# Layer 0's scores and queries as seven block products instead of eight (Strassen's form, float32)

## The chip, the core and the metric

The kernel runs on one core of a Trainium2 chip. The metric is device time in microseconds (us), the median of three runs. A core has five engines that run side by side, each its own queue in order: TensorE (PE in the profile) multiplies 128-wide blocks into PSUM, VectorE (DVE) and ScalarE (ACT) work element by element and can read PSUM, GpSimd (POOL) works on SBUF and reduces across partitions, SyncE (SP) issues transfers. They wait for each other by semaphores. All data here is float32.

## The reference, cut to what matters

Two attention layers on eight images of 1024 tokens and 256 channels:

```python
# layer 0: four heads, each 256 wide
qkv = einsum('bnc,cd->bnd', x, W_qkv)             # per head: q, k, v
atten = softmax(einsum('bihd,bjhd->bijh', q, k) * 256**-0.5, axis=j)
x = einsum('bijh,bjhd->bihd', atten, v) @ W_out + b_out + x
# layer 1: one head, keys and queries 32 wide, values 256 wide
f, g, h = x@Wf + bf, x@Wg + bg, x@Wh + bh
x = gamma * softmax(g @ f.T) @ h + x
```

## The kernel before

**Folding.** For each of layer 0's heads the kernel multiplies Wq by Wk transposed and Wv by W_out once (`fold_weights`). A query projection then gives Q = Wqk^T x^T, and the scores are x Q: the transposed tokens `x0T` serve as keys. The scores are kept transposed, keys on partitions and queries along the row.

**Blocks.** A head of an image is two blocks (`blk` 0 and 1) of 512 queries. A block's scores are eight key tiles of 128, each two products (channels 0 to 127 and 128 to 255) of 512 columns into one PSUM bank of the pool `ps_s`, four banks deep (L359). ScalarE copies each bank to the tile `s` (L367). VectorE takes the maximum over the key tiles (L373, L381, L383), GpSimd takes it across partitions (`partition_all_reduce`, L385), VectorE subtracts it in two instructions of 2048 elements (L388), and ScalarE takes the exponential (L391). Two blocks later, `values` multiplies the exponentials with V, four tasks of eight products of 257 columns (the last is the row sum, L402), and VectorE divides and adds to the rows (L410, L412). V has a column of ones, which GpSimd writes by a memset (L243).

**Order.** The heads of an image run one after the other; layer 1 of image b-1 stands after head 1 of image b (for the last image, after head 3), and layer 1 of the last image stands at the end. TensorE's order is fixed by `weave`, which spreads lists of tasks evenly over each other: a block's scores, the values of two blocks ago, and `coming`, the next head's preparation (transposes, folding, queries, V). The other engines' instructions are ordered by a scheduler, and each of their queues runs in that order. Loads of x go out on SyncE's queue, loads of weights on ScalarE's.

**Pools.** `sb1`, `sb2` and `sb3` give each tag one, two or three buffers; a tile waits until the readers of the tile whose buffer it takes are done. The rows x, the transposed xT, V and `s` have three, the queries q two.

Of the kernel before, what the change touches and what calls it, by code (L numbers as in the profile page):

```python
# [11 lines left out]
F32 = mybir.dt.float32  # L12
# [9 lines left out]
def kernel(  # L22
# [40 lines left out]

    nc = tc.nc
# [19 lines left out]
    sb3 = ctx.enter_context(tc.tile_pool(name="sb3", bufs=3))  # L84
    small = ctx.enter_context(tc.tile_pool(name="small", bufs=8))
# [8 lines left out]
    def load_x(b):  # L94
        t = sb3.tile([P, NT, C], F32, tag="rows", name=f"x_{b}")
        for k in range(NBLK):
            nc.sync.dma_start(
                t[:, ts(k, HT), :].rearrange("p t c -> p (t c)"), x_v[b][:, k, :]
            )
        rows[b] = t  # L100
# [36 lines left out]
    weights = {}  # L137

    def load_weights(h):
        w = sb1.tile([P, CC, 3 * C], F32, tag="wqkv", name=f"wqkv{h}")  # L140
        nc.scalar.dma_start(w, wqkv_v[:, :, ts(h, 3 * C)])
        wo = sb1.tile([P, CC, C], F32, tag="wout", name=f"wout{h}")
        nc.scalar.dma_start(wo, wout_v[:, ts(h, CC), :])
        weights[h] = w, wo

    def fold_weights(h):

        wT = []
        folded[h] = []

        def turn(i, what):
            w, _ = weights[h]
            pt = ps_m.tile([P, NB], F32, tag="pm", name=f"pw{what}_{h}")
            for d in range(CC):
                for c in range(CC):
                    nc.tensor.transpose(
                        pt[:, d * C + c * P : d * C + (c + 1) * P],
                        w[:, c, i * C + d * P : i * C + (d + 1) * P],
                        ident,
                    )  # L160
            t = sb1.tile([P, CC, C], F32, tag=f"w{what}T", name=f"w{what}T_{h}")
            copy_on(i, t.rearrange("p d c -> p (d c)"), pt)
            wT.append(t)

        def multiply(i, what):
            wqT, wkT, wvT = wT
            pm = ps_m.tile([P, NB], F32, tag="pm", name=f"p{what}_{h}")
            for c in range(CC):
                for d in range(CC):
                    nc.tensor.matmul(  # L170
                        pm[:, ts(c, C)],
                        lhsT=(wqT, wvT)[i][:, d, ts(c, P)],
                        rhs=wkT[:, d, :] if i == 0 else weights[h][1][:, d, :],
                        start=(d == 0),
                        stop=(d == CC - 1),
                    )
            t = const.tile([P, CC, C], F32, tag=f"{what}{h}", name=f"{what}{h}")
            copy_on(i, t.rearrange("p c e -> p (c e)"), pm)
            folded[h].append(t)

        tasks = [partial(turn, i, what) for i, what in enumerate(("q", "k", "v"))]
        tasks += [partial(multiply, i, what) for i, what in enumerate(("wqk", "wvo"))]
        return tasks


    xT_of = {}

    def transpose_rows(b, layer):


        def task(k, c):
            if (b, layer) not in xT_of:
                xT_of[b, layer] = sb3.tile([P, CC, N], F32, tag="xT", name=f"x{layer}T_{b}")
            pt = ps_m.tile([P, NB], F32, tag="pm", name=f"px{layer}_{b}_{k}_{c}")
            for t in range(HT):
                nc.tensor.transpose(  # L196
                    pt[:, ts(t, P)], rows[b][:, k * HT + t, ts(c, P)], ident
                )
            copy_on(c, xT_of[b, layer][:, c, ts(k, NB)], pt)

        return [partial(task, k, c) for k in range(NBLK) for c in range(CC)]
# [39 lines left out]
    def values_tile(name):  # L241
        v = sb3.tile([P, NT, CV], F32, tag="v", name=name)
        nc.gpsimd.memset(v[:, :, C : C + 1], 1.0)  # L243
        return v

    class Layer0:
        scale = SCALE

        def __init__(self, b, h):
            self.b, self.h, self.name = b, h, f"{b}_{h}"  # L250
            self.kchunks, self.together = CC, 1
            self.s = {}

        def start(self):
            self.q = sb2.tile([P, CC, N], F32, tag="q", name=f"q_{self.name}")
            self.v = values_tile(f"v_{self.name}")
# [11 lines left out]
        def prepare(self):  # L268
            b, h = self.b, self.h
            tasks = [self.start]  # L270
            if h == 0:
                tasks += transpose_rows(b, 0)
            if h not in folded:
                tasks += fold_weights(h)
            tasks += project_T(
                f"q_{self.name}", lambda: folded[h][0], C, lambda: xT_of[b, 0],
                lambda d, k, pm: copy_on(d, self.q[:, d, ts(k, NB)], pm),
            )
            tasks += project_rows(
                f"v_{self.name}", lambda: folded[h][1], lambda: xT_of[b, 0], self.store_v  # L280
            )
            return tasks

        def keys(self, c, j):
            return xT_of[self.b, 0][:, c, ts(j, P)]

        def queries(self, c, j, blk):
            return self.q[:, c, ts(blk, NB)]
# [4 lines left out]
    class Layer1:  # L293
        scale = 1.0

        def __init__(self, b):
            self.b, self.name = b, f"{b}_l1"
            self.kchunks, self.together = 1, P // CK
            self.s = {}

        def start(self):
            b = self.b
            self.f = sb1.tile([P, N], F32, tag="f", name=f"f_{b}")
            self.g = sb1.tile([P, N], F32, tag="g", name=f"g_{b}")
            self.v = values_tile(f"v_{self.name}")
# [8 lines left out]
        def prepare(self):  # L314
            b = self.b
            tasks = [self.start] + transpose_rows(b, 1)
            tasks += project_T(
                f"fg_{b}", lambda: wfg_sb, P, lambda: xT_of[b, 1], self.store_fg
            )
            tasks += project_rows(  # L320
                f"v_{self.name}", lambda: wh_sb, lambda: xT_of[b, 1],
# [5 lines left out]
            return tasks  # L327

        def keys(self, c, j):
            r = j % (P // CK)  # L330
            return self.f[ts(r, CK), ts(j, P)]

        def queries(self, c, j, blk):
            r = j % (P // CK)
            return self.g[ts(r, CK), ts(blk, NB)]
# [8 lines left out]
    def scores(a, blk):  # L344
        n = f"{a.name}_{blk}"
        half = NT // 2
        quart = NT // 4
        m = []

        def task(j0):  # L350
            if j0 == 0:
                a.s[blk] = sb3.tile([P, NT, NB], F32, tag="s", name=f"s_{n}")
            s = a.s[blk]
            js = range(j0, j0 + a.together)
            pms = {}
            for j in js:
                pms[j] = ps_s.tile([P, NB], F32, tag="ps", name=f"ps_{n}_{j}")
                for c in range(a.kchunks):
                    nc.tensor.matmul(  # L359
                        pms[j],  # L360
                        lhsT=a.keys(c, j),
                        rhs=a.queries(c, j, blk),
                        start=(c == 0),
                        stop=(c == a.kchunks - 1),
                    )
            for j in js:
                nc.scalar.copy(s[:, j, :], pms[j])  # L367
                if j % half == half - 1:
                    lo = j + 1 - half
                    t = sb1.tile(  # L370
                        [P, quart, NB], F32, tag=f"m{len(m)}", name=f"m{len(m)}_{n}"
                    )
                    nc.vector.tensor_tensor(  # L373
                        t, s[:, lo : lo + quart, :], s[:, lo + quart : lo + half, :], ALU.max
                    )
                    m.append(t)
            if js[-1] == NT - 1:
                softmax(s)

        def softmax(s):  # L380
# [5 lines left out]
            for k in range(2):  # L386
                part = s[:, ts(k, half), :]
                nc.vector.tensor_tensor(  # L388
                    part, part, cmax.unsqueeze(1).broadcast_to([P, half, NB]), ALU.subtract
                )  # L390
                nc.scalar.activation(part, part, AF.Exp, scale=a.scale)  # L391

        return [partial(task, j) for j in range(0, NT, a.together)]
# [42 lines left out]
    weave(order[0].prepare())  # L436
    due = []
    for i, a in enumerate(order):
        if isinstance(a, Layer0):
            if a.b == 0 and a.h + 1 < HEADS:  # L440
                load_weights(a.h + 1)
            if a.h == 1 and a.b + 1 < B:
                load_x(a.b + 1)
        coming = order[i + 1].prepare() if i + 1 < len(order) else []
        for blk in range(NBLK):
            n = len(coming) // NBLK
            now = values(*due.pop(0)) if len(due) == 2 else []
            weave(scores(a, blk), now, coming[blk * n : len(coming) if blk else n])
            due.append((a, blk))
    weave(values(*due[0]), final.prepare())  # L450
    weave([t for blk in range(NBLK) for t in scores(final, blk)])
# [36 lines left out]
```

## Time and profile before

| | |
|---|---|
| median of 3 runs | 2645.35 us (2644.98 to 2645.82) |
| the profiled execution | 2644.62 us |
| its span (first to last instruction) | 2642.7 us |
| mean granted TensorE clock | 0.998 |
| TensorE busy | 2609.2 us, 9648 products (each float32 product counts twice) |
| VectorE busy | 1072.0 us |
| ScalarE busy | 757.8 us |
| GpSimd busy | 150.1 us |
| layer 0's score products (L359) | 943.5 us |
| layer 0's query products (L210) | 239.1 us |
| layer 0's values products (L402) | 931.4 us |

The profile is of one execution. A row of its list of costliest groups names the line, the engine, the operation, the tiles out<-in, the shape and count; then come the busy time and the mean duration of one in ns, and after the second bar the time that the engine stood idle just before these instructions, with what ended that wait. TensorE's products overlap, so the busy time of a group is less than count times mean; the distance between starts in the timeline gives the rate. PE is the products, PEld the weight loads beside them. A row of the timeline gives start, duration and the instructions merged into it. "issue" is time in which an engine waited for nothing that the profile shows.

### The profile page before, as it was taken

What the parts mean: (1) busy time and instruction counts of PE and PEld (TensorE: products, weight loads), DVE (VectorE), ACT (ScalarE), POOL (GpSimd) and SP (SyncE); (2) the same over time, 40 slices, a digit from 0 to 9 for tenths busy, and PEclk for the clock granted to TensorE, in tenths of its full rate; (3) what the DMA queues carried; (4) which work ended last, traced back from release to release, by engine and by line L of the source; (5) the groups of instructions that cost most, each with busy time, mean ns of one, the idle gap of its engine ahead of it and who ended that gap; (6) DMA issues with size and microseconds to landing.
All of it is one profiled execution on the core that took longest, in us unless ns stands there. A gap on an engine that the chain in (4) does not pass through costs nothing.

```text
span 2642.7 us, 22461 instructions
## 1 busy us (share of the span) xinstructions
PE 2609.2 (99%) x9648; PEld 1772.3 (67%) x9648; DVE 1072.0 (41%) x1373; ACT 757.8 (29%) x985; POOL 150.1 (6%) x126
## 2 busy tenths in 40 slices
PE   7999999999999999999999999999999999999998
PEld 4666666666666666766667666676666766666676
DVE  2333335433354343433444343453334533333453
ACT  2322223322332223322233222332223322222332
POOL 0000000000000000000000000000000000000000
PEclk9999999999999999999999999999999999999999
DMA  3000000000000000000000000000000000000000
GB/s 105 17 0 0 0 1 1 8 24 0 1 0 9 24 1 0 1 8 24 0 1 0 8 24 0 0 1 32 0 0 1 1 16 0 1 0 1 0 1 32
DMA packets 8866, 23.06 MB, mean 9 GB/s; under 512 B 2112, under 2 KB 3648, under 8 KB 8768
## 3 DMA queue, kind: packets, MB, share of 16 engines
q1 hardware_dynamic: 6592, 17.44, 1.8%
q10 hardware_dynamic: 2176, 4.19, 0.5%
q8 instruction: 76, 1.25, 0.2%
q14 instruction: 22, 0.18, 0.0%
HBM read 13.24 MB, written 8.39 MB: 8 GB/s over the span
## 4 chain that ended last, share of the span: by engine, by line
PE 95%; DVE 2%; ACT 1%; POOL 1%; issue 1%; POOLq 0%; ACTq 0%
PE ps L359 33%; PE pa L402 32%; PE pr_v L230 8%; PE pa_l L402 8%; PE pm_q L210 8%; PE pr_v_l L230 2%; PE px L196 1%; DVE s_l L388 1%; PE pm_fg L210 1%; PE ps_l L359 1%; ACT s_l L367 1%; POOL cmax_l L385 1%; ACT s_l L391 1%; DVE m_l L381 0%; DVE m_l L373 0%
## 5 line engine op out<-in xcount | busy, mean ns | idle before, releaser
L359 PE MATMUL ps<-q,x0T 128*128 128x512 f32 x2048 | 943.5, 592 | 0.0
L402 PE MATMUL pa<-v,s 128*128 128x257 f32 x4096 | 931.4, 381 | 0.7 <-DVE x L412 0.7
L402 PEld LDWEIGHTS pa<-v,s 128*128 128x128 f32 x4096 | 776.7, 190 | 210.5 <-issue 112.9
L359 PEld LDWEIGHTS ps<-q,x0T 128*128 128x128 f32 x2048 | 385.3, 190 | 349.6 <-issue 332.3
L367 ACT COPY s<-ps 128x512 f32<-128x512 f32 x512 | 297.6, 582 | 1047.2 <-PE ps L359 1046.9
L388 DVE TENSOR_TENSOR s<-s,cmax 128x2048 f32<-128x2048 f32 x128 | 287.6, 2289 | 113.8 <-POOL cmax L385 113.8
L391 ACT ACTIVATE s<-s 128x2048 f32<-128x2048 f32 x128 | 244.8, 1913 | 290.1 <-DVE s L388 290.1
L410 DVE RECIPROCAL r<-pa 128x1 f32<-128x1 f32 x256 | 42.4, 165 | 619.0 <-PE pa L402 619.0
L373 DVE TENSOR_TENSOR m<-s 128x1024 f32<-128x1024 f32 x128 | 156.8, 1225 | 244.5 <-ACT s L367 244.5
L230 PE MATMUL pr_v<-wvo,x0T 128*128 128x256 f32 x1024 | 242.1, 380 | 2.9 <-ACT q L133 2.9
L402 PE MATMUL pa_l<-v_l,s_l 128*128 128x257 f32 x1024 | 233.8, 384 | 7.4 <-DVE x L412 7.4
L210 PE MATMUL pm_q<-x0T,wqk 128*128 128x512 f32 x512 | 239.1, 592 | 0.0
L230 PEld LDWEIGHTS pr_v<-wvo,x0T 128*128 128x128 f32 x1024 | 194.3, 190 | 62.9 <-issue 32.5
L402 PEld LDWEIGHTS pa_l<-v_l,s_l 128*128 128x128 f32 x1024 | 196.5, 192 | 57.4 <-issue 32.3
L385 POOL PARTITION_ALL_REDUCE cmax<-smax x64 | 115.6, 1806 | 1248.1 <-DVE smax L383 1197.0
L210 PEld LDWEIGHTS pm_q<-x0T,wqk 128*128 128x128 f32 x512 | 97.4, 190 | 91.3 <-issue 87.4
L412 DVE SCALAR_TENSOR_TENSOR x<-pa,r,x 128x256 f32<-128x256 f32 x256 | 123.8, 483 | 8.5
L410 DVE RECIPROCAL r_l<-pa_l 128x1 f32<-128x1 f32 x64 | 10.6, 167 | 215.4 <-PE pa_l L402 215.4
L367 ACT COPY s_l<-ps_l 128x512 f32<-128x512 f32 x128 | 65.9, 606 | 79.8 <-PE ps_l L359 79.8
L391 ACT ACTIVATE s_l<-s_l 128x2048 f32<-128x2048 f32 x32 | 61.2, 1912 | 94.0 <-DVE s_l L388 93.7
L388 DVE TENSOR_TENSOR s_l<-s_l,cmax_l 128x2048 f32<-128x2048 f32 x32 | 71.9, 2288 | 23.1 <-POOL cmax_l L385 23.1
L381 DVE TENSOR_TENSOR m<-m,m 128x1024 f32<-128x1024 f32 x64 | 78.4, 1225 | 2.2
(53 smaller groups left out, 780.4 us busy)
## 6 DMA issues: line engine op xcount, KB each, us to landing
x<-in_x_dram SPq DMA_DIRECT2D x16, 512.0 KB, 4.4
out_dram<-x SPq DMA_DIRECT2D x16, 512.0 KB, 2.6
wqkv<-in_L_conv_W_qkv_dram ACTq DMA_DIRECT2D x4, 768.0 KB, 4.4
wout<-in_L_conv_W_out_dram ACTq DMA_DIRECT2D x4, 256.0 KB, 2.7
wh_sb<-in_L_conv_Wh_dram SPq DMA_DIRECT2D x1, 256.0 KB, 2.8
bout_sb<-in_L_conv_b_out_dram SPq DMA_DIRECT2D x1, 128.0 KB, 7.2
bh_sb<-in_L_conv_bh_dram SPq DMA_DIRECT2D x1, 128.0 KB, 3.7
wfg_sb<-in_L_conv_Wf_dram SPq DMA_DIRECT2D x2, 32.0 KB, 6.6
```

Of the source, the lines that this page charges most:

```text
L210: nc.tensor.matmul(pm[:m], lhsT=w()[:, c, d * P : d * P + m], rhs=src()[:, c, ts(k, NB)], start=(c == 0), stop=(c == CC - 1),)
L230: nc.tensor.matmul(pm[:, ts(j, C)], lhsT=src()[:, c, ts(2 * t2 + j, P)], rhs=w()[:, c, :], start=(c == 0), stop=(c == CC - 1),)
L359: nc.tensor.matmul(pms[j], lhsT=a.keys(c, j), rhs=a.queries(c, j, blk), start=(c == 0), stop=(c == a.kchunks - 1),)
L367: nc.scalar.copy(s[:, j, :], pms[j])
L373: nc.vector.tensor_tensor(t, s[:, lo : lo + quart, :], s[:, lo + quart : lo + half, :], ALU.max)
L381: nc.vector.tensor_tensor(m[0], m[0], m[1], ALU.max)
L385: nc.gpsimd.partition_all_reduce(cmax, smax, P, bass_isa.ReduceOp.max)
L388: nc.vector.tensor_tensor(part, part, cmax.unsqueeze(1).broadcast_to([P, half, NB]), ALU.subtract)
L391: nc.scalar.activation(part, part, AF.Exp, scale=a.scale)
L402: nc.tensor.matmul(pm[:, : C + 1], lhsT=p[:, j, ts(ti, P)], rhs=v[:, j, : C + 1], start=(j == 0), stop=(j == NT - 1),)
L410: nc.vector.reciprocal(r, pm[:, C : C + 1])
L412: nc.vector.scalar_tensor_tensor(acc, pm[:, :C], r, acc, ALU.mult, ALU.add)
```

## The change

The products of layer 0's scores and queries are computed by Winograd's variant of Strassen's method. Both operands are cut into four blocks (tokens in halves and channels in halves; for the queries of a block, halves of 256), some sums of blocks are formed, seven block products are taken instead of eight, and the four output blocks are sums of these.

- `seven` is a group of three TensorE tasks. "one" takes products 1, 6 and 5 into three banks x, y and z; "two" adds product 2 to x and 7 to y; "three" adds product 4 to y and 3 to z. Between them ScalarE copies x (e1), and VectorE forms u2 and u3 from y and e1 and writes the outputs 22, 21 and 12 from a bank and e1, u2 or u3; output 11 is a ScalarE copy of x. A bank that gets a further product is read before it, so that product waits for the reader.
- A score block has two groups, each of two key tiles per half (28 products of 256 columns in all); a query projection is one group of products of 512 columns.
- The sums of operands are made on GpSimd: `sum_a` once an image on the transposed tokens (four instructions of 512 elements), `sum_b` once a head on the folded weights (128 elements) and once an image and head on the queries (512 elements).
- The maxima are taken per group (`Softmax.have`), and the subtraction and exponential go in four quarters of 1024 elements instead of two halves.
- The next head's queries run in the middle of block 1, V of a head is computed in its own two blocks, weights of all heads are loaded at the start into buffers of `s`, and heads 0 and 1 are folded before the first scores, 2 and 3 within the first block.
- The rows, xT and V have two buffers instead of three; x of the next image is loaded at head 3 instead of head 1.

```diff
-    def load_weights(h):
-        w = sb1.tile([P, CC, 3 * C], F32, tag="wqkv", name=f"wqkv{h}")
...
+    def load_weights(pair):
+        t = sb3.tile([P, NT, NB], F32, tag="s", name=f"w_{pair}").rearrange("p j i -> p (j i)")
...
+    def sum_a(eng, sums, a11, a12, a21, a22):
+        s1, s2, s3, s4 = sums
+        eng.tensor_tensor(s1, a21, a22, ALU.add)
+        eng.tensor_tensor(s2, s1, a11, ALU.subtract)
+        eng.tensor_tensor(s3, a11, a21, ALU.subtract)
+        eng.tensor_tensor(s4, a12, s2, ALU.subtract)
+
+    def sum_b(eng, sums, b11, b12, b21, b22):
+        t2, t3, t4 = sums
+        eng.tensor_tensor(t3, b22, b12, ALU.subtract)
+        eng.tensor_tensor(b12, b12, b11, ALU.subtract)
+        eng.tensor_tensor(t2, b22, b12, ALU.subtract)
+        eng.tensor_tensor(t4, b21, t2, ALU.subtract)
+
+    def seven(name, parts, operands, outs, after=None):
...
+        def bank(k):
+            banks[k] = ps_s.tile([P, NB], F32, tag="ps", name=f"ps{k}_{name}")
...
+        def add(dst, k, other):
+            nc.vector.tensor_tensor(dst, shaped(banks[k]), shaped(other), ALU.add)
+
+        def one():
+            for k, number in (("x", 1), ("y", 6), ("z", 5)):
+                bank(k)
+                product(k, number, True)
+            nc.scalar.copy(scratch("e1"), banks["x"])
+            add(shaped(scratch("u2")), "y", sbs["e1"])
+
+        def two():
+            product("x", 2)
+            product("y", 7)
+            nc.scalar.copy(outs["11"](), shaped(banks["x"]))
+            add(shaped(scratch("u3")), "y", sbs["e1"])
+            add(outs["22"](), "z", sbs["u3"])
+
+        def three():
+            product("y", 4)
+            product("z", 3)
+            add(outs["21"](), "y", sbs["e1"])
+            add(outs["12"](), "z", sbs["u2"])
+            if after is not None:
+                after()
+
+        return [one, two, three]
...
+            if layer == 0 and (k, c) == (NBLK - 1, CC - 1):
+                xT = xT_of[b, 0]
+                sums = sb2.tile([P, 4, HN], F32, tag="xs", name=f"xs_{b}")
...
+                sum_a(nc.gpsimd, (s1, s2, s3, s4), a11, a12, a21, a22)
...
     def values_tile(name):
-        v = sb3.tile([P, NT, CV], F32, tag="v", name=name)
+        v = sb2.tile([P, NT, CV], F32, tag="v", name=name)
         nc.gpsimd.memset(v[:, :, C : C + 1], 1.0)
...
+        def queries(self):
...
+            def after():
+                sums = sb2.tile([P, 3, NBLK, HB], F32, tag="qs", name=f"qs_{self.name}")
...
+                sum_b(nc.gpsimd, [sums[:, k] for k in range(3)], *blocks)
...
+        def have(self, pairs):
+
+            s, m, n = self.tile(), self.m, self.n
+            t = sb1.tile([P, 2, NB], F32, tag=f"m{len(m)}", name=f"m{len(m)}_{n}")
+            nc.vector.tensor_tensor(t, *[s[:, lo:hi, :] for lo, hi in pairs], ALU.max)
+            m.append(t)
+            if len(m) < 2:
+                return
             nc.vector.tensor_tensor(m[0], m[0], m[1], ALU.max)
...
             nc.gpsimd.partition_all_reduce(cmax, smax, P, bass_isa.ReduceOp.max)
-            for k in range(2):
-                part = s[:, ts(k, half), :]
+            for k in range(4):
+                part = s[:, ts(k, NT // 4), :]
...
+            fill = [values(*due.pop(0)) if len(due) == 2 else []]
+            n = len(own) // NBLK
+            fill.append(own[n:] if blk else own[:n])
+            if blk == 0:
+                fill.append(early)
+            elif isinstance(nxt, Layer0):
+                n = len(main) // 2
+                main = main[:n] + queries + main[n:]
+            else:
+                fill.append(queries)
+            weave(main, *fill)
             due.append((a, blk))
```

## The prediction

> **What bounds the kernel now.** I read the page's busy times first, then the chain that ended last, the costliest groups, and last the timelines of one stretch and of the start.
>
> ```profile
> PE 2609.2 (99%) x9648; PEld 1772.3 (67%) x9648; DVE 1072.0 (41%) x1373; ACT 757.8 (29%) x985; POOL 150.1 (6%) x126
> PE 95%; DVE 2%; ACT 1%; POOL 1%; issue 1%; POOLq 0%; ACTq 0%
> L359 PE MATMUL ps<-q,x0T 128*128 128x512 f32 x2048 | 943.5, 592 | 0.0
> L402 PE MATMUL pa<-v,s 128*128 128x257 f32 x4096 | 931.4, 381 | 0.7 <-DVE x L412 0.7
> L388 DVE TENSOR_TENSOR s<-s,cmax 128x2048 f32<-128x2048 f32 x128 | 287.6, 2289 | 113.8 <-POOL cmax L385 113.8
> L373 DVE TENSOR_TENSOR m<-s 128x1024 f32<-128x1024 f32 x128 | 156.8, 1225 | 244.5 <-ACT s L367 244.5
> ```
>
> TensorE is the bound: 95% of the chain, and 0.0 and 0.7 us idle before its two large groups. VectorE waits for others, so its order has cost nothing so far.
>
> The timeline of a score block, TensorE:
>
> ```profile
> 1048.12 3.63 PE L402 MATMUL pa<-v,s 128*128 128x257 f32 x16
> 1051.59 1.88 PE L359 MATMUL ps<-q,x0T 128*128 128x512 f32 x4
> 1053.30 1.88 PE L210 MATMUL pm_fg<-x1T,wfg_sb 128*128 128x512 f32 x4
> ...
> 1060.20 1.89 PE L230 MATMUL pr_v_l<-wh_sb,x1T 128*128 128x256 f32 x8
> 1061.93 3.60 PE L359 MATMUL ps<-q,x0T 128*128 128x512 f32 x8
> ```
>
> Start to start, a values task takes 3.47 us, four instructions of 512 columns 1.72, eight of 256 columns 1.73. A float32 product is two instructions: 0.86 us for 512 columns, 0.43 for 256. Halving the width costs nothing, so seven products for eight do save an eighth.
>
> VectorE and GpSimd in the softmax of that block:
>
> ```profile
> 1046.76 1.22 DVE L381 TENSOR_TENSOR m<-m,m 128x1024 f32<-128x1024 f32 x1
> 1048.02 0.69 DVE L383 TENSOR_TENSOR smax<-m 128x512 f32<-128x512 f32 x1
> 1049.04 1.16 DVE L312 COPY f<-f 64x512 f32<-64x512 f32 x1 [0.32 <-ACT f L311]
> 1050.90 4.50 DVE L388 TENSOR_TENSOR s<-s,cmax 128x2048 f32<-128x2048 f32 x2 [0.71 <-POOL cmax L385]
> 1055.43 0.42 DVE L312 COPY g<-g 64x512 f32<-64x512 f32 x1
> ```
>
> smax ends at 1048.71 and VectorE is free of the subtractions only at 1055.4. What stands behind them, in order, waits; here TensorE never needs it soon.
>
> GpSimd at the start:
>
> ```profile
> 0.87 0.19 POOL L243 MEMSET v<- 128x8 f32 x3
> 11.78 0.28 POOL masks.py:199 TENSOR_SCALAR_AFFINE_SELECT ident<-ident 128x128 f32<-128x128 f32 x1 [10.72 <-issue]
> ```
>
> The program has a library load of GpSimd between these two; the gap is 10.72 us.
>
> [...] The trace has 10.72 us, but from 2 to 8 us the DMA engines stood at 0.9 to 1.0 busy with the first loads. [...]
>
> **The change, part by part.**
>
> Removed: each of 64 score blocks runs 28 products of 256 columns for 16 of 512: two units of 0.86, 64 x 1.72 = 110.1 us. Each of 32 query projections runs seven for eight: 27.5 us. Sum 137.6 us of TensorE time. It is real only where TensorE doesn't wait.
>
> Added on VectorE: five PSUM sums per group of seven, five groups per head, 800 in all, at 690 ns (the row of L262, the nearest) 552 us, less 64 query copies (44 us). 1072 + 508 is about 1580 us in 2640: capacity is there. ScalarE loses copies. Neither is the bound on average; what counts is order.
>
> Where TensorE now waits: a group's tasks are "one" (2.58 us), "two" (1.72), "three" (1.72). "three" begins with product 4, accumulated into bank y, and so waits for u3, a VectorE sum. VectorE's stream has, in most blocks, u2 of the next block's first group, then the last maxima, smax, the four subtractions, and only then u3. So product 4 waits for the previous block's whole softmax. Take t=0 where the last values task before a block's end ends. After a matmul's slot VectorE starts 0.21 us later (30.73 to 30.94 at the start).
> TensorE: three to 1.72, one to 4.30, values to 7.77, two to 9.49; in block 1 a V projection (1.72) follows and product 4 is due at 11.2; in block 0 a values task, due at 12.96.
> VectorE: output 21 from 1.07 to 1.76, output 12 from 1.93 to 2.62, maximum (1.23) to 3.88, u2 to 4.6, maximum to 5.84, smax to 6.56. All-reduce from 6.73 (0.17 later, as in the trace) to 8.55 (1.8). Four subtractions (4.5 to 4.9) to 13.35. Reciprocal, u3 to 14.25; product 4 starts at 14.3. Then output 22, a values update and the exposed weight load (190 ns) add 0.5 to 0.8 before product 3.
> Wait: 3.6 us on entering block 1 (14.3 - 11.2 + 0.5), 2.0 on entering block 0.
>
> GpSimd's reloads: the sums (tensor_tensor) and the all-reduce are in two libraries. The built program's GpSimd stream has 39 loads ahead of an all-reduce and 38 back; before has one each. The loads back hide: the query sums wait for mid-block-1 anyway. The others don't. In block 1 the queue reads: four query sums, memset of the next V tile, load, all-reduce. V has two buffers now, so the memset waits for the last values task, t=0. The load starts near 0.3 and the all-reduce at 0.3+L in place of 6.73. At L=6 it is covered; at L=8 it costs 1.6 us; at 10.7, 4.3. This happens at 31 entries into a Layer-0 block 0.
> At seven heads (h=3, another image to come) four x sums stand ahead of block 0's all-reduce. Three of them follow the last transposed copy (t=0.8)[...], then the load[...].
>
> L is the unknown: [...] 10.7 (trace, DMA full). In mid-kernel the DMA is idle (8 GB/s)[...]. I take 8.
> Waits at L=8: 25 x 3.6 = 90, 7 x 10.1 = 71, 31 x 3.6 = 112; sum 273.
> Start: queries now wait for x sums, weight sums and query sums[...], against folds done early: +8. Seven entries into Layer 1, with copies queued behind exponentials: +10. [...]
> Span: 2642.7 - 137.6 + 273 + 28 = 2806. The profiled execution took 2644.6, 1.9 over its span, and the median is 0.7 above that: 2809 us.
>
> Costed at nothing: loading x(b+1) at h=3, not h=1. The last output of the shared buffer leaves after t=0.9; by the trace's spacing (out issued to x landed, 6.3 us) x lands near 7.7, when the transposes are due, and any excess falls into the wait for u3. Two buffers for xT: the copies wait for readers a head ago. Without the wait for u3 each would show at most 1 us, seven times. Early folds keep their TensorE time.
>
> **The rivals.**
> Short reload, L of 6.4 or less: 90 + 7 x 8.1 + 31 x 2.0 = 209; with 28, 2745 us (free of all reload cost 2703). [...] against: 10.72 in the trace.
> Long reload, L=10.7: 90 + 7 x 12.8 + 31 x 6.3 = 375[...]: 2943 us, 2946 as median. For it: the only measured load of this kernel. Against: DMA load then.
> Faster: the softmax chain ends inside TensorE's cover. Place: product 4 against u3; price: no wait, 2642.7 - 137.6 + 18 = 2523, 2526 as median. It decides once the mean wait over 63 entries is under 1.9 us (119.6 / 63). For it: cover of 11.2 to 13 us is close to 14.3. Against: the reloads, and every link of the chain is a measured row.
> Change without effect: products don't shrink to seven eighths. Excluded by 1.72 and 1.73 above.
>
> **How the numbers follow.** Forecast (L 6.5 to 9.5, 2750 to 2880) 0.45; long reload 0.27; short or free 0.21; faster 0.05; waits that eat just the gain 0.02. This kernel's measurement tells about 0.2% (5 us) from no change. So faster 0.05, same 0.02, slower 0.93. The range runs from between free and short reload, 2715, to the long one, 2950; outside lie the faster and equal cases, part of the free one and a longer reload: under 0.2.
>
> **What would show it.** Score products at seven eighths of their busy time (about 825 us) and queries (about 209), both on L191; TensorE idle before psy released by VectorE L208 of 200 to 375 us; a gap on GpSimd of 6 to 11 us before L533 after each memset, which gives L directly; longest waits at h=3; VectorE near 1580 us. The forecast is wrong if all-reduces start right after smax at block 0 (L under 6.4), or if u3 runs ahead of the subtractions.

## The result and the profile after

The changed kernel takes 2684.97 us (median of 4 runs, 2683.93 to 2687.31), the kernel before beside it 2645.59 (2644.98 to 2645.93): a ratio of 1.015, 95% interval 1.0133 to 1.0168. The profiled execution has a span of 2682.4 us and a granted clock of 0.985. So it is slower, as forecast, but by 39 us and not by 164, and it lies below the forecast's range.

The page after, its main lines:

```profile
PE 2522.3 (94%) x11120; PEld 2058.9 (77%) x11120; DVE 1560.6 (58%) x2269; ACT 635.4 (24%) x889; POOL 364.2 (14%) x302
PE 69%; DVE 21%; POOL 4%; issue 2%; ACT 2%; DMA 1%; POOLq 0%; DVEq 0%; SPq 0%; ACTq 0%
L536 DVE TENSOR_TENSOR s<-s,cmax 128x1024 f32<-128x1024 f32 x256 | 296.4, 1220 | 140.6 <-POOL cmax L533 140.6
L191 PE MATMUL psy<-qs,x0T 128*128 128x256 f32 x512 | 142.9, 403 | 115.1 <-DVE u L208 104.3
L525 DVE TENSOR_TENSOR m<-s 128x1024 f32<-128x1024 f32 x128 | 161.5, 1262 | 13.1 <-DVE s L208 0.5
```

TensorE's busy time fell by 86.9 us (2609.2 to 2522.3), but its idle time rose by 126.6 (33.5 to 160.1 of the span): together the 39.7 us of the spans. VectorE went from 2% of the chain to 21%. One row holds nearly all of the new idle time: `psy<-qs,x0T`, product 4 of the group of seven, 115.1 us ahead of it. Taken one by one, these are: 7 waits of 7.3 to 7.5 us (52 in all), 17 of 2.28 (39), 31 of 0.5 to 1.1 (24).

One of the 17, at the entry to a block 1 (from the timeline; the prediction's t=0 is at 194.83):

```profile
199.30 1.22 DVE L529 TENSOR_TENSOR m<-m,m 128x1024 f32<-128x1024 f32 x1
200.55 0.69 DVE L531 TENSOR_TENSOR smax<-m 128x512 f32<-128x512 f32 x1
201.34 1.78 POOL L533 PARTITION_ALL_REDUCE cmax<-smax  x1 [26.83 <-DVE smax L531]
203.16 4.63 DVE L536 TENSOR_TENSOR s<-s,cmax 128x1024 f32<-128x1024 f32 x4 [1.92 <-POOL cmax L533]
204.34 1.89 PE L336 MATMUL pr_v<-wvo,x0T 128*128 128x256 f32 x8
207.78 0.67 DVE L208 TENSOR_TENSOR u<-psy,e 128x512 f32<-128x512 f32 x1
208.51 1.13 PE L191 MATMUL psy<-qs,x0T 128*128 128x256 f32 x4 [2.28 <-DVE u L208]
```

This is the forecast's chain link by link: maxima, all-reduce, four subtractions, and only then u3, with product 4 behind it. TensorE's projection would have let it start at 204.34 + 1.72 = 206.06; it starts at 208.51, t = 13.68.

One of the seven, at the fourth head, where another image comes (t=0 is 265.11):

```profile
268.67 2.13 POOL L169 TENSOR_TENSOR xs<-x0T,xs 128x512 f32<-128x512 f32 x1
271.92 0.69 DVE L531 TENSOR_TENSOR smax<-m 128x512 f32<-128x512 f32 x1
276.82 1.80 POOL L533 PARTITION_ALL_REDUCE cmax<-smax  x1 [6.02 <-issue]
278.66 4.63 DVE L536 TENSOR_TENSOR s<-s,cmax 128x1024 f32<-128x1024 f32 x4 [4.87 <-POOL cmax L533]
283.21 0.69 DVE L208 TENSOR_TENSOR u<-psy,e 128x512 f32<-128x512 f32 x1
283.95 2.07 PE L191 MATMUL psy<-qs,x0T 128*128 128x256 f32 x4 [7.43 <-DVE u L208]
```

The sums of x end at 270.80, and then GpSimd stands for 6.02 us with nothing to wait for. The waits of the page put it at 41.8 us in 7 times, 6.1 at most. That is the reload L, measured.

The stretch behind this wait, in steps of 2 us (after the times: length, busy time and instructions of PE, PEld, DVE, ACT and POOL, then TensorE's granted clock, the DMA share and GB/s):

```profile
280.00:282.00 2.00, 0.00 (x0) 0.00 (x0) 2.00 (x2) 2.00 (x3) 0.00 (x0) 0.95 0.00 0
282.00:284.00 2.00, 0.05 (x1) 0.05 (x1) 1.97 (x4) 2.00 (x3) 0.00 (x0) 0.50 0.00 0
284.00:286.00 2.00, 2.00 (x5) 1.64 (x6) 0.62 (x1) 0.38 (x1) 0.00 (x0) 0.50 0.00 0
286.00:288.00 2.00, 2.00 (x7) 1.55 (x6) 0.93 (x2) 0.00 (x0) 0.00 (x0) 0.50 0.00 0
288.00:290.00 2.00, 2.00 (x9) 1.74 (x8) 1.68 (x2) 0.00 (x0) 0.00 (x0) 0.84 0.00 0
```

From about 281.8 to 288.6 the clock is half. Two us of it fall into the wait, the rest slows work: products 4 and 3 fill 3.57 us where their slot is 1.73. All such dips of the span add up to about 40 us of lost clock ((1 - 0.985) x 2682), against 5 before.

### The profile page after: what moved, and what is told of

Read it like the earlier page. It is cut to its first block, busy times and chain, and to the rows that moved or that the text cites. A ratio compares the mean times of both kernels' runs of the same rounds, so it can differ in the third digit from the quotient of the medians.

```text
span 2682.4 us, 26798 instructions
## 1 busy us (share of the span) xinstructions
PE 2522.3 (94%) x11120; PEld 2058.9 (77%) x11120; DVE 1560.6 (58%) x2269; ACT 635.4 (24%) x889; POOL 364.2 (14%) x302
## 4 chain that ended last, share of the span: by engine, by line
PE 69%; DVE 21%; POOL 4%; issue 2%; ACT 2%; DMA 1%; POOLq 0%; DVEq 0%; SPq 0%; ACTq 0%
PE pa L549 24%; PE psy L191 10%; DVE s L536 8%; PE psz L191 7%; PE pr_v L336 7%; PE pa_l L549 5%; PE psx L191 5%; POOL cmax L533 3%; PE psy_q L191 3%; DVE u L208 2%; PE psz_q L191 2%; PE psx_q L191 2%; DVE s_l L536 2%; DVE m L529 2%; DVE m L525 1%
## 5 line engine op out<-in xcount | busy, mean ns | idle before, releaser
L536 DVE TENSOR_TENSOR s<-s,cmax 128x1024 f32<-128x1024 f32 x256 | 296.4, 1220 | 140.6 <-POOL cmax L533 140.6
L540 ACT ACTIVATE s<-s 128x1024 f32<-128x1024 f32 x256 | 260.2, 1055 | 359.4 <-DVE s L536 358.8
L191 PE MATMUL psz<-q,xs 128*128 128x256 f32 x1024 | 272.7, 390 | 0.0
L191 PE MATMUL psx<-q,x0T 128*128 128x256 f32 x1024 | 263.5, 380 | 3.9 <-ACT s_l L497 3.9
L191 PE MATMUL psy<-qs,xs 128*128 128x256 f32 x1024 | 263.5, 380 | 3.6 <-POOL qs L175 3.6
L191 PE MATMUL psy<-qs,x0T 128*128 128x256 f32 x512 | 142.9, 403 | 115.1 <-DVE u L208 104.3
L208 DVE TENSOR_TENSOR u<-psy,e 128x512 f32<-128x512 f32 x256 | 175.3, 685 | 125.4 <-PE psy L191 124.1
L191 PEld LDWEIGHTS psz<-q,xs 128*128 128x128 f32 x1024 | 196.4, 194 | 34.5 <-DVE s L208 7.7
L191 PEld LDWEIGHTS psx<-q,x0T 128*128 128x128 f32 x1024 | 191.6, 190 | 36.9 <-ACT s_l L497 8.9
L191 PEld LDWEIGHTS psy<-qs,xs 128*128 128x128 f32 x1024 | 194.7, 190 | 30.5 <-POOL qs L175 4.0
L191 PEld LDWEIGHTS psy<-qs,x0T 128*128 128x128 f32 x512 | 95.1, 197 | 144.7 <-DVE u L208 100.0
L208 DVE TENSOR_TENSOR s<-psz,u 128x512 f32<-128x512 f32 x256 | 176.6, 690 | 28.3 <-PE psz L191 24.8
```

The costliest lines, as they stand in the source:

```text
L191: nc.tensor.matmul(banks[k][:, ts(i, NB // parts)], lhsT=lhsT, rhs=rhs, start=first and i == 0, stop=True, skip_group_check=True,)
L208: nc.vector.tensor_tensor(dst, shaped(banks[k]), shaped(other), ALU.add)
L536: nc.vector.tensor_tensor(part, part, cmax.unsqueeze(1).broadcast_to([P, NT // 4, NB]), ALU.subtract,)
L540: nc.scalar.activation(part, part, AF.Exp, scale=self.a.scale)
```

## The experiments

Theory: the loss is one of order. Product 4 stands behind the previous block's softmax because u3 stands behind the subtractions on VectorE; take that away, and the products' saving shows. Rival: GpSimd's sums and reloads make the loss (by arriving late, or by slowing VectorE beside them).

### The subtractions put behind u3

```diff
-    ctx.enter_context(tc.manual_schedule(engines={mybir.EngineType.PE}))
+    ctx.enter_context(tc.manual_schedule(engines={mybir.EngineType.PE, mybir.EngineType.DVE}))
...
             add(outs["22"](), "z", sbs["u3"])
+            flush()
...
-            for k in range(4):
+            def finish():
+                for k in range(4):
...
+            pending.append(finish)
```

`flush` runs the subtractions and exponentials of the block before; in layer 1 it stands ahead of the maxima.

> VectorE's order alone is changed: the four subtractions of a block stand behind u3 and output 22 of the next block's first group. Order theory (product 4 waits for u3, which stands behind the previous block's subtractions): the waits go, 25 x 2.45 + 31 x 0.9 = 89 us and at the seven heads with x sums most of 7 x 10 = 70 us, so 2520 to 2560 us, under the kernel before. GpSimd theory (the sums and library loads on GpSimd cost the time, wherever VectorE stands): little changes, 2640 us or more. Capacity theory (VectorE is too full): 2660 or more.

Measured 2562.26 us, ratio 0.9688 (0.9674 to 0.9702). This is two us above the order theory's range and 122.7 below the changed kernel; the kernel with this order is 3.1% faster than before. The GpSimd theory's 2640 or more and the capacity theory's 2660 or more are both excluded. The fourth head of this kernel:

```profile
272.72 0.69 DVE L213 TENSOR_TENSOR u<-psy,e 128x512 f32<-128x512 f32 x1 [1.02 <-PE psy L196]
274.25 1.03 PE L196 MATMUL psy<-qs,x0T 128*128 128x256 f32 x4
274.67 1.80 POOL L540 PARTITION_ALL_REDUCE cmax<-smax  x1 [5.97 <-DVE s L213]
276.50 4.63 DVE L545 TENSOR_TENSOR s<-s,cmax 128x1024 f32<-128x1024 f32 x4 [2.36 <-POOL cmax L540]
```

GpSimd is as late as ever (the 5.97 us gap is still there), but u3 no longer waits for it, and product 4 starts with no wait at all.

### A control: VectorE's order by hand, nothing deferred

The first line of the diff above alone.

> Control for the deferral: the changed kernel with VectorE's instructions in the order of the program and nothing deferred, so the subtractions still stand ahead of the next block's first sums. If the deferral made the gain: no gain here, 2675 to 2710. If writing VectorE's order by hand made it: below 2620.

Measured 3014.11 us, 1.1394 (1.1377 to 1.1411). This is far outside both ranges. In program order, and not deferred, the subtractions stand ahead even of u2, so product 7 of the group, earlier than product 4, already waits for the softmax; from the waits of TensorE:

```profile
PE psy L191 <- DVE u L208: 311.8, 63, 10.2
```

So the gain of the first run came from the deferral and not from the hand order. This run also shows what the scheduler's order was worth to the changed kernel, where u2 stands ahead of the last maxima: in program order the same instructions cost 329 us more, with a granted clock of 0.935.

### GpSimd's sums moved behind the all-reduce

The sums of the next image's x run in block 1, after block 0's all-reduce, with GpSimd in program order; the second run has the deferral too.

```diff
-            if layer == 0 and (k, c) == (NBLK - 1, CC - 1):
+            if layer == 0 and b == 0 and (k, c) == (NBLK - 1, CC - 1):
+                x_sums(b)
...
+                if nxt.h == 0:
+                    main = main[:1] + [partial(x_sums, nxt.b)] + main[1:n] + queries + main[n:]
```

> The x sums go behind the all-reduce of block 0 of head 3, next to the query sums, and GpSimd runs in the order of the program; 64 library loads in place of 78, subtractions still ahead of u3. Order theory: only the seven long waits shrink, from about 10 us with the slow clock to 2.5: minus 52, so 2630 us (2620 to 2645). GpSimd theory: the library loads are the cost, 2600 us or less.

> Both edits. Order theory: once u3 no longer waits for the subtractions, where the x sums stand matters little: 2515 to 2550 us, at most 15 us below the first of these runs. GpSimd theory: about the sum of a small gain from the order and a large one from the loads, so clearly (over 30 us) below the run with the order alone.

> GpSimd alone runs in the order of the program: the memset of V stands behind the all-reduce, so the library load at the entries to a block 0 no longer waits for the last values task; the x sums stay where they are. If the load was already covered there (about 6 us, ready when smax is): no change, 2680 to 2690 us. If it was exposed by over a us at 31 entries: 2650 us or less.

The last is their control: GpSimd in program order and nothing else. Measured: 2653.49 (1.0028, 1.0015 to 1.004) with the sums late, 2567.92 (0.9707, 0.9693 to 0.9722) with both, 2703.36 (1.022, 1.0205 to 1.0235) for the control. All three missed their ranges, by 8.5, 17.9 and 13.4 us; the GpSimd theory's figures for the first two are missed by more.

With the sums late the seven long waits shrink from 7.4 to 2.81 us:

```profile
280.74 1.53 PE L191 MATMUL psy<-qs,x0T 128*128 128x256 f32 x4 [2.81 <-DVE u L208]
```

That is 7 x 4.6 = 32 us, and the run is 31.5 below the changed kernel; the forecast of 52 had counted about 10 us for each wait with its slow clock. The control went the other way. In program order the sum that needs only early copies no longer runs ahead of the last copy, so all four sums follow it:

```profile
283.77 1.80 POOL L533 PARTITION_ALL_REDUCE cmax<-smax  x1 [6.54 <-issue]
290.90 2.07 PE L191 MATMUL psz<-q,xs 128*128 128x256 f32 x4 [9.30 <-DVE s L208]
```

The all-reduce starts 14.4 us after t=0 (269.33 there) in place of 11.7, and seven waits grow from 7.4 to about 8.9 us (here u3 runs ahead of the subtractions, and product 3 waits for the sum that reads its bank, behind them). That is 10 us, and the clock falls from 0.985 to 0.981; together they cover the 18.4 us by which the control is slower. Against this control, moving the sums is worth 49.9 us. With the deferral it is worth nothing (5.7 us slower). So GpSimd's lateness is a real part of the loss, 32 us against the changed kernel, but only through a sum's place behind the subtractions (u3's, in the control the next one's).

### The sums of x on VectorE

```diff
-                sum_a(nc.gpsimd, (s1, s2, s3, s4), a11, a12, a21, a22)
+                sum_a(nc.vector, (s1, s2, s3, s4), a11, a12, a21, a22)
```

> The changed kernel with the four sums of x on VectorE in place of GpSimd, nothing else: no sums and no 6.0 us gap ahead of the all-reduce at the fourth head, but up to 2.8 us of sums ahead of the maxima on VectorE. GpSimd term (the 6.0 us gap and the sums make the fourth head's long wait): that wait falls from 7.5 to 3.5 to 4.5 us, 7 times, and the slower clock behind it shortens, 2685 - 25 - 10 = 2650, range 2640 to 2665. If the wait there comes from VectorE's queue alone: 2680 to 2705.

Measured 2661.94 us, 1.0066 (1.0049 to 1.0083), 23.0 below the changed kernel and inside the GpSimd term's range. The long waits are now 3.37 us, seven times:

```profile
280.56 1.13 PE L191 MATMUL psy<-qs,x0T 128*128 128x256 f32 x4 [3.37 <-DVE u L208]
```

7 x (7.4 - 3.4) = 28 us of waits went. A later text calls this run e10.

### The two halves of the change, one at a time

Queries by seven with scores by eight (each bank copied out by ScalarE), and the reverse:

```diff
+            def task(j):
+                pm = ps_s.tile([P, NB], F32, tag="ps", name=f"ps_{n}_{j}")
+                for c in range(CC):
+                    nc.tensor.matmul(
+                        pm,
+                        lhsT=xT_of[self.b, 0][:, c, ts(j, P)],
+                        rhs=self.q[:, c, ts(blk, NB)],
...
+                nc.scalar.copy(soft.tile()[:, j, :], pm)
```

```diff
+            def task(d, k):
+                pm = ps_s.tile([P, NB], F32, tag="ps", name=f"pq_{self.name}_{d}_{k}")
+                for c in range(CC):
+                    nc.tensor.matmul(
+                        pm,
+                        lhsT=folded[h][0][:, c, ts(d, P)],
+                        rhs=xT_of[b, 0][:, c, ts(k, NB)],
...
+                copy_on(d, dst, pm.unsqueeze(1))
```

> Changed kernel with the queries alone by seven products; the scores are eight products again, each bank copied out by ScalarE, so no later product waits for a sum on VectorE within a block; the sums of x stay on GpSimd ahead of the all-reduce, the sums of q are gone. Order theory (the loss comes only where a score product waits for a sum that stands behind the softmax): nearly the whole queries' term is kept, 2645 - 27.5 + about 5 at the start = 2623, range 2615 to 2635, and no wait over 2 us for VectorE at the entry to the fourth head. GpSimd theory (the late all-reduce costs by itself): the 7 entries still cost about 50 to 70 us, 2670 to 2690.

> Changed kernel with the scores alone by seven products; the queries are eight products again, the sums of x and of q stay. Terms add up: the changed kernel's 2685 plus the queries' 27.5, less some 0 to 8 us of waits of the queries at the start, 2704 to 2713. If the queries' products cost more by their waits than they save: below 2690.

Queries alone: 2648.92 us, 1.0015 (1.0008 to 1.0022). The all-reduce of the fourth heads is as late here (41.8 us of gaps in 7 times), yet no wait there is over 1 us; so its lateness alone does not cost 50 us, and the GpSimd theory's range is missed. But the order theory's is missed too, by 14 us: the 27.5 us of the queries do not show. TensorE's named waits after its first product are 34.2 us against 16.8 before, among them 8 for `u_q` (6.8 us) and 8 for `e_q` (6.4, of which 3.6 once early on). That accounts for 17 of the 31 us between 27.5 saved and 4.0 lost. Counted from start to start, an image's query products take 26.3 us in mid-run, against 27.6 before; seven eighths would be 24.1. What remains isn't placed.

Scores alone: 2731.12 us, 1.0323 (1.0308 to 1.0339), 46 above the changed kernel and 18 above the range. The waits ahead of product 4 are the same as in the changed kernel, 116.0 us to 115.2. What differs is the clock, 0.977 to 0.985. Here is one entry to a block 1 in the kernel with the scores alone, and the windows of 2 us behind it (columns as above):

```profile
212.09 1.50 PE L191 MATMUL psy<-qs,x0T 128*128 128x256 f32 x4 [2.28 <-DVE u L208]
```

```profile
212.00:214.00 2.00, 1.91 (x6) 1.55 (x7) 1.40 (x4) 0.93 (x2) 0.00 (x0) 0.68 0.00 0
214.00:216.00 2.00, 2.00 (x6) 1.22 (x5) 0.98 (x2) 0.00 (x0) 0.00 (x0) 0.50 0.00 0
216.00:218.00 2.00, 2.00 (x8) 1.20 (x7) 1.72 (x3) 0.00 (x0) 0.00 (x0) 0.97 0.00 0
```

The same wait of 2.28 us that left the clock alone at 208.51 in the changed kernel halves it here for 3.4 us, which costs 1.7. In this kernel it does so behind 13 of the 17 such waits, in the changed kernel behind none: 13 x 1.7 = 22 us, enough for the 18. The last section says what differed between the two.

### The best version, and what the queries are worth in it

Three more kernels build on the first run. In one, two waits of the hand order go: the scaling of a bias that waits for a load moves behind the first stage, and the last flush behind the last but two groups of value products.

```diff
-        nc.vector.tensor_scalar(bh_sb, bh_sb, gamma_sb, None, ALU.mult)
+    def scale_bias():
+        nc.vector.tensor_scalar(bh_sb, bh_sb, gamma_sb, None, ALU.mult)
...
+    scale_bias()
...
-    flush()
     weave(values(*due[1]))
+    flush()
```

> The deferred kernel with two waits of its hand order on VectorE taken away: the scaling of the value bias (which waits for a load until 21.8 us) moved behind the first stage, so the second transpose no longer waits 10 us for it, and the last deferred subtractions moved behind the last but two groups of value products, so 10.1 us for a reciprocal go. Order theory: 2562 - 5 - 10 = about 2547, range 2540 to 2555. If these waits lie beside others: 2555 to 2562.

Measured 2552.87 us, 0.9651 (0.9635 to 0.9667): 9.4 us less, inside the range. The next two texts call this kernel e7. The second takes it with the queries by eight:

> The kernel of e7 (subtractions deferred, the two waits gone) with the queries by eight products again, so it tells what the seven of the queries are worth where the scores no longer wait. If their term holds there: 2553 + 27.5 = 2580, range 2573 to 2585. If their small waits eat most of it, as where the queries alone were changed: 2553 to 2562.

Measured 2555.65 us, 0.9663 (0.9648 to 0.9677): the queries' seven are worth 2.8 us here. From one image to the next the two kernels' values tasks drift apart by 1.0 us, where 4 x 0.86 = 3.4 are saved; and the first values task comes 3.6 us later with seven, since two early query products wait for sums (0.9 and 3.9 us). Most of the other 2.4 us of an image stand in this stretch of the kernel with seven:

```profile
580.27 1.80 POOL L542 PARTITION_ALL_REDUCE cmax<-smax  x1 [5.97 <-DVE s L215]
582.10 4.63 DVE L547 TENSOR_TENSOR s<-s,cmax 128x1024 f32<-128x1024 f32 x4 [2.36 <-POOL cmax L542]
587.25 0.68 DVE L215 TENSOR_TENSOR s<-psz,u 128x512 f32<-128x512 f32 x1
587.39 1.12 PE L198 MATMUL psz_q<-xs,wqk 128*128 128x512 f32 x2 [0.47 <-DVE s L215]
589.78 0.68 DVE L215 TENSOR_TENSOR u_q<-psy_q,e_q 128x512 f32<-128x512 f32 x1
590.51 1.12 PE L198 MATMUL psy_q<-xs,wt 128*128 128x512 f32 x2 [1.04 <-DVE u_q L215]
```

The reload of 5.97 us shows again: the deferred subtractions are late by it, now stand ahead of the sums that free the queries' banks, and two query products wait (0.47 and 1.04 us). The third kernel tests that, with the sums of x on VectorE:

> The kernel of e7 (subtractions deferred) with the four sums of x on VectorE as in e10. In e7 the late all-reduce of the fourth head puts the deferred subtractions ahead of the sums that two query products wait for, some 2.3 us for each of 7 or 8 images. If that is where the queries' saving went: no such wait, 2553 - 17 = 2536, range 2532 to 2545. If the queries' waits have another cause: 2549 to 2556.

Measured 2544.98 us, 0.9621 (0.9605 to 0.9637): 7.9 us less, at the upper edge of its range, and in its trace no query product waits for VectorE after the start. But 17 us were forecast: the waits for sums that free the scores' bank z rose from 5.5 to 8.8 us, and the rest of the difference isn't placed. This is the fastest kernel, 3.8% faster than before.

## Why the prediction was right in kind and wrong in size

- **Product time.** Four instructions of 256 columns start 0.86 us apart, as priced, and the first deferred run shows that most of the saving is there to take. The check named for it was a bad one: the L191 rows of the scores add up to 942.6 us (not 825) and of the queries to 231 (not 209), because the modelled busy time of a group of four is 1.03 us in a slot of 0.86; groups overlap, and smaller groups count more overlap.
- **The wait: product 4 behind u3 behind the previous block's softmax.** Right in place and cause; shown by the timeline and by the deferral.
- **The size of this wait, the step that failed most.** In block 1 the forecast put product 4 at 14.3, which is 3.1 us behind its due time of 11.2, and added 0.5 for what follows: 3.6 us, 25 times. Measured: due 11.23, start 13.68, so 2.45 (2.28 of it idle), and product 3 follows 0.99 us later in place of 0.86, so the add-on is 0.13. The 0.6 us gather over the links: smax ends 0.15 us earlier than forecast, the subtractions 0.39, u3 0.63. VectorE overlaps its instructions a little: u3 starts at 207.78, when the subtractions (203.16 + 4.63) are just ending, although a reciprocal (207.71 to 207.87) lies between them. This holds for 17 entries. At the other eight (seven heads that layer 1 follows, and the first head) there is no wait of note: at one of the seven (t=0 at 411.21) TensorE has a values task more ahead of product 4, which is due at 14.7, and u3 ends at 14.15. The forecast gave all 25 the short cover. At the entries to block 0 the 2.0 us that it had without the load's delay became 0.5 to 1.1.
- **L = 8, the step that failed next.** It measured 6.0 us. The 8 was the author's estimate, under the 10.72 us of the start because the DMA engines were busy there (0.90 to 1.03 from 2 to 8 us). In the trace after, the start's gap is 9.65 us, with the DMA engines 0.75 to 1.03 busy in that stretch; that its length was the DMA's doing wasn't tried. At 6.0 the load behind the memset is just covered: at one entry to block 0 (t=0 at 166.10) the all-reduce starts at 172.71, t = 6.6, and at all of them within 0.2 us of the end of smax, which the forecast had named as a sign of being wrong.
- **What each was worth.** The waits were forecast at 273 us and measured at 115. In the forecast's own terms L = 8 in place of 6 is 31 x 1.6 + 7 x 2.0 = 64 us of the difference; the other 94 are the links and the eight entries without a wait. The largest single miss, the 31 entries to block 0 (112 us forecast, 24 measured), is 50 us of L and 38 of the links.
- **Seven fourth heads, 10.1 us each.** The 6.5 us of these for the late all-reduce (10.1 - 3.6) were the author's estimate; no trace of before has a sum on GpSimd. The wait was 7.6 us from due to start; of the 2.5 too many, 2.0 are L. Behind each wait 4.7 to 5.2 us of work ran at half clock, which lost 2.3 to 2.6 us and brings the cost back to 10, but that is luck: the forecast had the clock as a term of its own.
- **Start +8, layer 1 +10, clock +10.** The first score product starts at 41.3 in place of 35.9, and two waits of 3.6 and 3.7 us follow. No wait of layer 1's entries stands out in TensorE's list. The clock's 10 us, like the 45 within the long reload's 2943, were the author's estimate. The clock lost 35 us more than before, a part of it inside waits. Before has such losses too: TensorE's waits there include 4.1, 3.4 and 4.0 us in the last 95 us, and the 4.6 us of clock that before lost are there.
- **The terms put at nothing.** The two buffers and the later load of x stayed at nothing: between the start and the last image's layer 1, TensorE's list names no wait for a DMA or for a transposed copy, in the changed kernel or in the deferred one.
- **The sum.** Idle time took 126.6 us more than before; 115.2 us stand at these entries, where 273 was forecast. TensorE's busy time fell by 86.9 and not by 137.6. In the fastest kernel, which has few waits, it fell by 117.0; so about 30 of the missing 50.7 us go with the waits (half clock among them), and 20 do not, which isn't split further. Without this term the 126.6 us would have been less than the 137.6 saved: that the kernel came out slower at all is in part luck.
- **The rivals.** The short reload was the true case, yet its 2745 us carried the waits of 3.6 and 2.0; even "free of all reload cost", 2703, was too high. The rival on the other side should have decided at a mean wait under 1.9 us over 63 entries. The mean idle time was 115.2 / 63 = 1.83, from due to start up to 0.2 more, so about at the threshold, and yet the kernel was 39 us slower: the threshold left out what a wait costs after it ends.

## What to carry over

When a product starts to depend on a sum on another engine, look at what the queue of that engine holds ahead of the sum, and move the long work that nobody needs soon (here the subtractions) behind it before judging the arithmetic. Where a wait is a small difference of two long chains, subtract two times of one timeline rather than adding rows: 14.3 for 13.7, with 0.5 for 0.13 behind it, made 3.6 us out of 2.6. After an edit that removes a wait, look for the next consumer on the same queue; the cost of the reload moved from the scores to the queries. And count what stands behind a wait: here the clock lost 35 us, partly behind the waits, where 10 were estimated.

## What the runs showed of the hardware

- The granted clock fell in units: in the changed kernel every half-clock stretch that ends within the span lasts 3.41 us (1.7 us lost), 6.83 or 10.24, and all of them start on one grid of 3.41 us (at 46.3, 83.8, 281.8 and 609.5 us and so on, which are 11, 58 and 96 steps apart). The same idle time of 2.28 us led to a dip 13 times of 17 in the kernel with the scores alone and never in the changed kernel.
- What differed between the two is where a wait fell on this grid. In the thirteen traces, past the first 25 us, 165 steps at full clock held 2.0 us or more of TensorE's idle time, and all of them were followed by a step at half clock; of 409 steps with 0.5 to 1.65 us none was; of the 70 between, 11 were (in the changed kernel alone: all 11 steps with 2.05 us or more, and none of the 75 with 0.5 to 1.99). At the 13 dips of the kernel with the scores alone, 1.90 us or more of the wait fell into one step; at its other four waits at most 1.76 did, and at the 17 of the changed kernel at most 1.81. These are counts over traces (the ends of products are modelled); no run moved a wait along the grid to try it.
- A sum of 512 float32 on GpSimd took 1.27 us, and the last of an image's four 2.13 at the seven fourth heads, where it ran beside two maxima on VectorE, which took 1.84 and 1.68 us there (1.23 and 1.22 at most other places).
- Where GpSimd changed from sums to the all-reduce in mid-kernel, it stood for 6.0 us (41.8 us in 7 times). It started this before the operand was there, so that it hid where the all-reduce was due later: at the entry to block 0 above, the all-reduce started 6.27 us after the memset and 0.2 us after smax ended.
